# Message steps woven into the last block's projections, with x2 stored by halves of its columns and engine shares set by phase

## The chip, the cores and the metric

The kernel runs on one core of one Trainium2 chip. The metric is the device time of one execution in microseconds; lower is better. A core has five engines that run in parallel, each with its own instruction queue: TensorE (PE, matmuls and transposes into PSUM), VectorE (DVE), ScalarE (ACT), GpSimd (POOL) and SyncE (SP), which here mostly issues DMAs. An instruction waits at the head of its engine's queue until what it needs is there, and everything behind it on that engine waits with it.

## The reference

Four images of 128x128 pixels with 128 channels, in fp32, go through four residual layers, each on a group-normalised input (32 groups of 4 channels):

```python
x = x + relu(deform_conv(gn(x), offset(gn(x)), w_def))          # layer 0
x = x + scan_layer(gn(x), W)                                    # layer 1
x = x + messages(gn(x), Wself, Wm, Wk)                          # layer 2
x = x + triangle(gn(x), ...)                                    # layer 3

# layer 1: over image rows, new = row + relu(conv1d(previous new, W of 9 taps))
# layer 2
z_self = einsum('bmkd,hd->bmkh', x, Wself)
z_m = einsum('bmd,hd->bmh', sum(x, axis=2), Wm)[:, :, None, :]
z_k = einsum('bkd,hd->bkh', sum(x, axis=1), Wk)[:, None, :, :]
out = z_self + z_m + z_k
# layer 3
xn = layer_norm(x)
left = (xn @ left_w + left_b) * sigmoid(xn @ lgate_w + lgate_b)
right = (xn @ right_w + right_b) * sigmoid(xn @ rgate_w + rgate_b)
out_gate = sigmoid(xn @ ogate_w + ogate_b)
out = einsum('bkjd,bkid->bijd', left, right)
out = (layer_norm(out, onorm_g, onorm_b) * out_gate) @ to_out_w + to_out_b
```

## The kernel before

Channels lie on the 128 partitions. The kernel is a sequence of stages. `deform_layer` does layer 0 and `scan_layer` does layer 1 for all four images (batches) together; in both, a scheduler decides the order of the instructions on each engine. `message_terms` then makes the small operands of layer 2. `last_layers` does layer 2's messages and layer 3 batch by batch; there the order is written out by hand: each engine runs its instructions in the order in which the Python code emits them.

**`scan_layer`** steps through the 128 rows of the images. For a row, PE transposes four 128x128 blocks of x1 (`x1T_ps`, L1064), ACT applies the norm (`rowT`, L1068), PE convolves the carried row in two halves of two batches each (`both_ps` L1099, `own_ps` L1104 and L1110), ACT copies `both_ps` to `shared` (L1124), and DVE forms `total` (L1126), the new carry (L1129), differences for the next row (L1078) and the layer's result `x2c` (L1136). After every fourth row, a boundary of which there are 32, DVE takes `bn_stats` (L1144) and row sums (L1148, `sum_w`), POOL adds column sums (L1150, `sum_h`), and ACT's queue issues one store per batch to the HBM tensor `x2T` (L1147), four rows of 128 columns for each partition.

**`message_terms`** folds layer 2's group norm, a scale s and a shift t for each channel and batch, into its operands: `ws` (Wself scaled, plus the identity for the residual) and `z`, the row and column terms of the messages.

**`last_layers`** keeps one batch in SBUF as `X` (128x128x128 fp32) and its projections in `T`. It is written as Python generators; each `yield` ends a step, and the main loop at its end calls them in turns:

- `messages(b)`: 16 steps of 8 rows. A step loads `x2c` from x2T (SP), has POOL add the row and column terms (`zc`, L1332), does two matmuls (L1345), and DVE adds them into X (L1349) and takes two `bn_stats` (L1354). Loads and zc are fetched two steps ahead; x2c and zc share four buffers.
- `scaled(b)`: statistics of X to the operands of the next norm; eight 1-MB stores of X to `x3T` (the residual for the end).
- `normed(b)`: 16 blocks of 8 rows, `centred` by two matmuls (L1435), with two ACT passes per block, the squares (L1441) and the centred X (L1444). For every 16 rows a generator `divided` turns the mean of squares into a standard deviation (L1401), sends it through HBM (`stdT`) to spread it over partitions, takes the reciprocal (L1409), stores it (L1411) and loads it again, broadcast to all partitions (`rwide`, L1417), in two halves; each half is multiplied into X by two DVE instructions of 128x512 (L1424). Each step of `normed` advances every open `divided` by one step.
- `multiplied(b, q)`, for the four quarters q of the channels (called q0 to q3): 16 projection steps (8 matmuls and every second time one for the gate; a sigmoid on ACT L1497; two multiplies on DVE L1500), then eight product steps (four matmuls L1519 and a copy by ACT L1523). A projection step reads eight of X's first-axis slices, in order; the gates go to HBM (`gateT`).
- `given_out(b)`: layer 3's output norm, gate and projection for the 32 groups of four columns, k from -6 to 32. It works two batches' stages at once: it belongs to batch b but runs between the steps of batch b+1. A full step has DVE statistics (L1546), now and then a group of `scales` (L1562 to L1570, with a square root on ACT L1568), four normalisations `u` (ACT L1615 or POOL L1613), four transposes (L1585), y on ACT (L1587), the gate multiply (L1588, on POOL, and on DVE for the last batch), eight matmuls (L1596, L1600), and a copy of the result by ACT (L1617). x3 and the gate come in and the result goes out by DMAs on SP's queue.

The main loop before: while messages(b) has steps, given_out takes eight; three in scaled; two in normed, whose last steps run into the first projections; 24 in the projections of q0 to q2; three in q3. Messages of batch b+1 begin at n = 15 in q3, where n counts the steps of `multiplied`:

```python
if q + 1 == NQ:
    if n < 6 and n % 2:
        step(out_of)
    if n == 15:
        if b + 1 < B:
            msgs = messages(b + 1)
            step(msgs)
    elif n > 16 and n % 2:
        step(msgs)
```

So four of 16 message steps lie beside q3's products, and 12 follow them. After the last batch's q3, given_out(3) runs alone.

Of the kernel before, what the change touches and what calls it, by code (L numbers as in the profile page):

```python
# [19 lines left out]
P = 128  # L20
B = 4
# [989 lines left out]
def scan_layer(tc, c, small, x1, w, norms, x2T):  # L1011
# [18 lines left out]
    with ExitStack() as ctx:  # L1030
# [55 lines left out]
        for y in range(S):  # L1086
# [54 lines left out]
            if i == RB - 1:  # L1141
                y0 = y + 1 - RB
                for b in range(B):
                    nc.vector.bn_stats(  # L1144
                        stats[:, b, y // RB, :], x2c[:, b].rearrange("p h w -> p (h w)")
                    )
                    nc.scalar.dma_start(x2T[b, :, y0 : y + 1, :], x2c[:, b])  # L1147
# [74 lines left out]
def message_terms(tc, c, keep, work, counted, w2, outb):  # L1222
# [4 lines left out]
    wself, wm, wk = w2  # L1227
    ws = keep.tile([P, B, P], F32, name="ws")
    z = keep.tile([P, 2, B, S], F32, name="z")
    with tc.tile_pool(name="l2ps", bufs=1, space=PSUM) as psum:  # L1230
# [17 lines left out]
        nc.vector.scalar_tensor_tensor(t, mean, -1.0, s, ALU.mult, ALU.mult)  # L1248
        for b in range(B):
            nc.vector.scalar_tensor_tensor(  # L1250
                ws[:, b], wself, s[:, b : b + 1], c.ident, ALU.mult, ALU.add
            )
        tsum = work.tile([P, B], F32, name="tsum")
        nc.vector.tensor_scalar(tsum, t, float(S), None, ALU.mult)
        msg = work.tile([P, 2, B, S], F32, name="msg")
        for n, sums in enumerate((sum_w, sum_h)):
            for by, op in ((s, ALU.mult), (tsum, ALU.add)):
                nc.vector.tensor_tensor(
                    msg[:, n], sums if op is ALU.mult else msg[:, n],
                    by.unsqueeze(2).to_broadcast([P, B, S]), op,  # L1260
                )
        twide = work.tile([P, B, S], F32, name="twide")
        nc.vector.tensor_copy(twide, t.unsqueeze(2).to_broadcast([P, B, S]))
        pm = psum.tile([P, B, S], F32, name="row_ps")
        nc.tensor.matmul(pm, lhsT=wm, rhs=msg[:, 0], start=True, stop=False)
        nc.tensor.matmul(pm, lhsT=wself, rhs=twide, start=False, stop=True)
        pk = psum.tile([P, B, S], F32, name="column_ps")
        nc.tensor.matmul(pk, lhsT=wk, rhs=msg[:, 1], start=True, stop=True)

        nc.vector.tensor_scalar(z[:, 0], pm, outb, None, ALU.add)  # L1270
        nc.scalar.copy(z[:, 1], pk)
# [3 lines left out]
def last_layers(tc, c, terms, w, x2T, out, x3T, gateT, stdT):  # L1275
# [9 lines left out]
    with ExitStack() as ctx:  # L1285
# [36 lines left out]
        def messages(b):  # L1322

            stats = xs[b] = one.tile([P, S // 4, 6], F32, name="stats3")
            got = []

            def fetch(y0):
                if y0 < S:
# [428 lines left out]
```

## Time and profile before

| | |
|---|---|
| median of 3 runs | 5456.43 us (5450.79 to 5477.0) |
| the profiled execution's own time | 5459.8 us |
| its span | 5458.1 us |
| layer 0 | 0 to 3120 us |
| scan layer | 3120 to 3952 us |
| message terms | 3952 to 3973 us |
| last layers | 3973 to 5458 us |
| in these, from the first messages of one batch to those of the next | 358 us (batches 1 to 2 and 2 to 3) |
| last batch's given_out alone | 5335 to 5458 us |

The profile is one execution; the span is what lies between its first and last instruction, and the remaining 1.7 us lie around it. Within one batch's period of 358 us (batch 1's q0 to batch 2's), the phases take 53 (q0), 57 (q1), 57 (q2), 47 (q3's projections), 63 (its products and the next messages), 30 (scaled) and 51 us (normed up to the first projection). A group of the profile gives a line, an engine and an operation, its operands and shape, how often it ran, its busy time and the mean ns of one, and after the second bar how long the engine stood idle just before it and for what. A line of the waits view gives the engine and line that waited, what it waited for, total us, times and the longest.

### The profile page before, as it was taken

The page shows a single profiled execution, that of the slowest core. Times are in us where ns is not written, and L with a number is a line of the kernel's source. Part 1 is how long each engine was busy: PE and PEld are TensorE (multiplying, and loading weights), DVE is VectorE, ACT ScalarE, POOL GpSimd, SP SyncE. Part 2 cuts the span into 40 slices and gives each one's busy share as a digit, 9 for nine tenths or more (in the row PEclk, how much of TensorE's full clock was granted, in tenths as well). Part 3 has the DMA queues.
Part 4 walks back from the last instruction along what each step waited for, and adds up shares of the span by engine and source line. Part 5 has one row for each costly group of instructions (what it writes and reads, how often), then busy time and mean ns, then how long its engine had stood idle before and what let it go on. Part 6 is the DMA issues. An engine that isn't in the chain of part 4 may idle for free. (4 is left out here: it accounts for less than half of the span.)

```text
span 5458.1 us, 162832 instructions
## 1 busy us (share of the span) xinstructions
PE 4887.5 (90%) x68890; PEld 4229.0 (77%) x68890; DVE 3237.4 (59%) x8389; ACT 2536.8 (46%) x5206; POOL 1137.0 (21%) x1013
## 2 busy tenths in 40 slices
PE   1898999999999998989999799999969699798897
PEld 1787788788888787877899699999928478396596
DVE  4676666666666655665545466666654654546445
ACT  1554454544554444545544233333234375573666
POOL 4222121210221201212100011111120232323222
PEclk9999998999999999999999899999989899899998
DMA  5776666665666665665644322222141553554535
GB/s 151 162 161 145 138 139 140 142 150 103 142 138 130 157 120 107 150 130 126 129 85 90 73 82 78 78 84 83 61 166 64 174 179 122 195 172 145 191 132 193
DMA packets 1273817, 710.67 MB, mean 130 GB/s; under 512 B 845645, under 2 KB 1112174, under 8 KB 1263862
## 3 DMA queue, kind: packets, MB, share of 16 engines
q1 hardware_dynamic: 1243538, 658.56, 47.8%
q10 hardware_dynamic: 29540, 41.60, 2.2%
q8 instruction: 545, 8.93, 0.7%
q14 instruction: 194, 1.59, 0.1%
HBM read 417.28 MB, written 282.55 MB: 128 GB/s over the span
## 5 line engine op out<-in xcount | busy, mean ns | idle before, releaser
L606 PE MATMUL conv_ps<-ring,wdef 128*128 128x192 f32 (+2 forms) x7632 | 1301.2, 320 | 8.7 <-DVE x1c L576 6.6
L514 DVE TENSOR_TENSOR m<-t_ps,tent 128x390 f32<-128x390 f32 x1548 | 806.7, 557 | 783.2 <-ACT tent L512 767.5
L606 PEld LDWEIGHTS conv_ps<-ring,wdef 128*128 128x128 f32 x7632 | 1146.9, 195 | 127.1 <-issue 64.6
L512 ACT COPY tent<-t_ps 128x390 f32<-128x390 f32 x1560 | 690.5, 487 | 654.7 <-PE t_ps L498 642.2
L498 PE MATMUL t_ps<-parts_of,spread 57*64 57x99 bf16 (+1 forms) x12384 | 742.5, 275 | 169.0 <-DVE m L514 149.3
L523 PE MATMUL v_ps<-m,pixels 60*64 60x108 f32 (+1 forms) x22704 | 812.5, 264 | 19.0 <-DVE m L514 11.1
L498 PEld LDWEIGHTS <-spread 57*64 57x64 bf16 x12480 | 578.7, 125 | 313.0 <-issue 265.7
L523 PEld LDWEIGHTS v_ps<-m,pixels 60*64 60x64 f32 x22704 | 673.0, 137 | 69.8 <-DVE m L514 24.7
L549 ACT COPY ring<-v_ps 128x432 f32<-128x432 f32 x1032 | 505.1, 525 | 445.7 <-PE v_ps L523 444.8
L420 POOL TENSOR_TENSOR off<-off,koff 72x512 f32<-72x512 f32 x128 | 162.7, 1271 | 1768.2 <-DVE off L417 1768.2
L1500 DVE TENSOR_TENSOR T<-pair_ps,sig 128x256 f32<-128x256 f32 x512 | 282.6, 594 | 390.8 <-ACT sig L1497 390.7
L1110 PEld LDWEIGHTS own_ps<-diff,wconv 128*128 128x128 f32 x4064 | 493.6, 191 | 13.1
L1492 PEld LDWEIGHTS pair_ps<-wcat,X 128*128 128x128 f32 x4096 | 472.7, 192 | 38.1 <-issue 29.1
L1110 PE MATMUL own_ps<-diff,wconv 128*128 128x128 f32 x4064 | 494.6, 273 | 0.0
L1492 PE MATMUL pair_ps<-wcat,X 128*128 128x128 f32 x4096 | 481.5, 276 | 5.2 <-DVE T L1500 3.1
L506 PE MATMUL t_ps<-parts_of,spread 57*64 57x130 bf16 x9288 | 454.5, 225 | 0.0
L1150 POOL TENSOR_TENSOR sum_h<-sum_h,x2c 128x512 f32<-128x512 f32 x128 | 162.4, 1268 | 1150.5 <-DVE x2c L1136 684.8
L438 DVE SCALAR_TENSOR_TENSOR parts<-off,parts 72x512 bf16<-72x512 f32 x384 | 296.1, 771 | 153.5 <-ACT parts L430 147.7
L1068 ACT ACTIVATE rowT<-x1T_ps,t_x,s_x 128x128 f32<-128x128 f32 x512 | 208.2, 571 | 323.2 <-PE x1T_ps L1064 320.8
L506 PEld LDWEIGHTS <-spread 57*64 57x64 bf16 x9312 | 318.9, 108 | 0.1
L1497 ACT ACTIVATE sig<-pair_ps 128x512 f32<-128x512 f32 x256 | 152.1, 598 | 253.5 <-DVE T L1500 104.6
L1099 PE MATMUL both_ps<-carry,wsum 128*128 128x128 f32 x2032 | 268.3, 273 | 1.1 <-DVE carry L1133 1.1
(195 smaller groups left out, 6609.8 us busy)
## 6 DMA issues: line engine op xcount, KB each, us to landing
pixels<-tab SPq DMA_DIRECT2D x688, 123.8 KB
parts_of<-off SPq DMA_DIRECT2D x1032, 55.7 KB
off<-parts SPq DMA_DIRECT2D x64, 891.0 KB
tab<-rows SPq DMA_DIRECT2D x384, 128.0 KB
xin<-in_x_dram SPq DMA_DIRECT2D x128, 256.0 KB
x<-x1c SPq DMA_DIRECT2D x32, 1024.0 KB
x1rows<-x SPq DMA_DIRECT2D x128, 256.0 KB
x2T<-x2c ACTq DMA_DIRECT2D x128, 256.0 KB
```

The source lines that it names most:

```text
L438: nc.vector.scalar_tensor_tensor(parts[:, NSPLIT + i, h : h + RO, 2 : S + 2], off, 0.0, part, ALU.is_gt, ALU.mult,)
L498: nc.tensor.matmul(tp[h : h + HALF, 0, 0:n].rearrange("p (r c) -> p r c", c=PADW)[:, :, i:PADW:RX], lhsT=spread[0:k, kx // 2, i, h : h + H ...
L506: nc.tensor.matmul(tp[h : h + HALF, 1, i * PADW : (i + 1) * PADW], lhsT=spread[HALF : HALF + k, kx // 2, first + i, h : h + HALF], rhs=src ...
L512: nc.scalar.copy(tent[:, 0:n], tp[:, 0, 0:n])
L514: nc.vector.tensor_tensor(m, *pair, ALU.mult)
L523: nc.tensor.matmul(to[p1 : p1 + HALF], lhsT=pix[p0 : p0 + LANES, xb, :], rhs=m[p0 : p0 + LANES, :, RX * xb : RX * xb + w], start=True, sto ...
L549: nc.scalar.copy(to, bodies[side])
L606: nc.tensor.matmul(pc[:, at : at + rows, x0:x1], lhsT=wdef[:, side, k, :], rhs=v[:, :, k if v.shape[2] == NK else kx, x0 + kx : x1 + kx], ...
L1099: nc.tensor.matmul(both, lhsT=wsum[:, j, :], rhs=old[h][:, 1, :, j : j + V], start=(j == 0), stop=(j == NJ - 1),)
L1110: nc.tensor.matmul(own[:, n], lhsT=wt[:, 2 * j + n, :], rhs=diffs[h][:, n, :, j : j + V], start=False, stop=(n == 1 and j == NJ - 1),)
L1492: nc.tensor.matmul(pj[:, j], lhsT=X[:, j0 + j, :], rhs=w.wcat[:, q * 4 * DQ : (q + 1) * 4 * DQ], start=True, stop=True,)
L1500: nc.vector.tensor_tensor(to, pj[:, :, e].rearrange("p j d -> p d j"), sig[:, :, e].rearrange("p j d -> p d j"), ALU.mult,)
```

## The change

`x2T` gets a further axis: [B, P, 2, S, S/2], so that each half of the columns lies together. Each store of `scan_layer` is split into two.

`message_terms` no longer scales the row and column sums. The scale goes into copies of the weights (per batch, Wm on POOL and Wk on ACT), the shift into one small matmul with `wshift` = S (Wm + Wk) + Wself, made at the start by `message_weights`. Results come per batch from one PSUM tile.

`messages(b)` steps over 16 rows x 64 columns, first half of X's first axis and then the second. Because q3's projections have passed the first half by then, messages of b+1 can start inside them: they are fetched at n = 7, eight steps run with n = 8 to 15 and three with n = 17, 20 and 23; five are left after q3.

`divided` waits one step more between the rwide loads and the multiplies, and the second multiply of each half goes to POOL. `centred` puts every second block's centred X on DVE. The loop of normed makes 25 steps before the projections, with given_out at 7, 15 and 23; given_out takes seven steps beside the messages, three in scaled and three in normed.

`given_out` always takes scales in groups of four columns' groups, a step before they are used, with statistics six steps ahead. The four `u` of a step are shared by phase: all on ACT up to k = 5 and two each on ACT and POOL later (before three and one); for the last batch one on ACT and three on POOL (before two and two).

```diff
-                    nc.scalar.dma_start(x2T[b, :, y0 : y + 1, :], x2c[:, b])
+                    for n in range(2):
+                        nc.scalar.dma_start(
+                            x2T[b, :, n, y0 : y + 1, :], x2c[:, b, :, n * V : (n + 1) * V]
+                        )
...
+def message_weights(tc, work, w2):
+
+    nc = tc.nc
+    wt = []
+    for v, name in zip(w2, ("wself", "wm", "wk")):
+        t = work.tile([P, P], F32, name=name)
+        nc.scalar.dma_start(t, v)
+        wt.append(t)
+    wself, wm, wk = wt
+    shifted = work.tile([P, P], F32, name="wshift")
+    nc.vector.tensor_tensor(shifted, wm, wk, ALU.add)
+    nc.vector.scalar_tensor_tensor(shifted, shifted, float(S), wself, ALU.mult, ALU.add)
+    return wself, wm, wk, shifted
...
+        same_ps = psum.tile([P, B], F32, name="same_ps")
+        nc.tensor.matmul(same_ps, lhsT=shifted, rhs=t, start=True, stop=True)
+        same = work.tile([P, B], F32, name="same")
+        nc.vector.tensor_scalar(same, same_ps, outb, None, ALU.add)
+        scaled = work.tile([P, B, 2, P], F32, name="wscaled")
         for b in range(B):
-            nc.vector.scalar_tensor_tensor(
-                ws[:, b], wself, s[:, b : b + 1], c.ident, ALU.mult, ALU.add
-            )
-        tsum = work.tile([P, B], F32, name="tsum")
-        nc.vector.tensor_scalar(tsum, t, float(S), None, ALU.mult)
-        msg = work.tile([P, 2, B, S], F32, name="msg")
-        for n, sums in enumerate((sum_w, sum_h)):
-            for by, op in ((s, ALU.mult), (tsum, ALU.add)):
-                nc.vector.tensor_tensor(
-                    msg[:, n], sums if op is ALU.mult else msg[:, n],
-                    by.unsqueeze(2).to_broadcast([P, B, S]), op,
-                )
-        twide = work.tile([P, B, S], F32, name="twide")
-        nc.vector.tensor_copy(twide, t.unsqueeze(2).to_broadcast([P, B, S]))
-        pm = psum.tile([P, B, S], F32, name="row_ps")
-        nc.tensor.matmul(pm, lhsT=wm, rhs=msg[:, 0], start=True, stop=False)
-        nc.tensor.matmul(pm, lhsT=wself, rhs=twide, start=False, stop=True)
-        pk = psum.tile([P, B, S], F32, name="column_ps")
-        nc.tensor.matmul(pk, lhsT=wk, rhs=msg[:, 1], start=True, stop=True)
-
-        nc.vector.tensor_scalar(z[:, 0], pm, outb, None, ALU.add)
-        nc.scalar.copy(z[:, 1], pk)
+            sb = s[:, b : b + 1]
+            nc.vector.scalar_tensor_tensor(ws[:, b], wself, sb, c.ident, ALU.mult, ALU.add)
+            nc.gpsimd.tensor_scalar(scaled[:, b, 0], wm, sb, None, ALU.mult)
+            nc.scalar.activation(scaled[:, b, 1], wk, AF.Copy, scale=sb)
+            pm = psum.tile([P, 2, S], F32, name="added_ps")
+            for n, sums in enumerate((sum_w, sum_h)):
+                nc.tensor.matmul(
+                    pm[:, n], lhsT=scaled[:, b, n], rhs=sums[:, b], start=True, stop=True
+                )
+            nc.vector.tensor_scalar(z[:, 0, b], pm[:, 0], same[:, b : b + 1], None, ALU.add)
+            nc.scalar.copy(z[:, 1, b], pm[:, 1])
     return ws, z
...
+            RB, V = 2 * JB, S // 2
...
+            todo = [(n, y0) for n in range(2) for y0 in range(0, S, RB)]
             got = []
 
-            def fetch(y0):
-                if y0 < S:
-                    x2c = four.tile([P, JB, S], F32, name="x2c", tag="wide")
-                    nc.sync.dma_start(x2c, x2T[b, :, y0 : y0 + JB, :])
-                    zc = four.tile([P, JB, S], F32, name="zc", tag="wide")
+            def fetch(i):
+                if i < len(todo):
+                    n, y0 = todo[i]
+                    x2c = four.tile([P, RB, V], F32, name="x2c", tag="wide")
+                    nc.sync.dma_start(x2c, x2T[b, :, n, y0 : y0 + RB, :])
+                    zc = four.tile([P, RB, V], F32, name="zc", tag="wide")
                     nc.gpsimd.tensor_tensor(
-                        zc, z[:, 0, b, y0 : y0 + JB].unsqueeze(2).to_broadcast([P, JB, S]),
-                        z[:, 1, b].unsqueeze(1).to_broadcast([P, JB, S]), ALU.add,
+                        zc, z[:, 0, b, y0 : y0 + RB].unsqueeze(2).to_broadcast([P, RB, V]),
+                        z[:, 1, b, n * V : (n + 1) * V].unsqueeze(1).to_broadcast([P, RB, V]),
+                        ALU.add,
                     )
                     got.append((x2c, zc))
 
             fetch(0)
-            fetch(JB)
+            fetch(1)
             yield
-            for y0 in range(0, S, JB):
+            for i, (n, y0) in enumerate(todo):
                 x2c, zc = got.pop(0)
                 pz = pair()
                 for h in range(2):
                     nc.tensor.matmul(
-                        pz[:, h], lhsT=ws[:, b], rhs=x2c[:, 4 * h : 4 * h + 4],
+                        pz[:, h], lhsT=ws[:, b], rhs=x2c[:, JB * h : JB * (h + 1)],
                         start=True, stop=True,
                     )
+                x = X[:, n * V : (n + 1) * V]
                 nc.vector.tensor_tensor(
-                    X[:, :, y0 : y0 + JB].rearrange("p w h -> p h w"),
-                    pz.rearrange("p n (h w) -> p (n h) w", w=S), zc, ALU.add,
-                )
-                for h in range(0, JB, 4):
+                    x[:, :, y0 : y0 + RB].rearrange("p w h -> p h w"),
+                    pz.rearrange("p n (h w) -> p (n h) w", w=V), zc, ALU.add,
+                )
+                for h in range(2):
                     nc.vector.bn_stats(
-                        stats[:, (y0 + h) // 4, :], X[:, :, y0 + h : y0 + h + 4]
-                    )
-                fetch(y0 + 2 * JB)
+                        stats[:, 2 * i + h, :], x[:, :, y0 + JB * h : y0 + JB * (h + 1)]
+                    )
+                fetch(i + 2)
                 yield
...
                     rws.append((j1, rw))
                 yield
-                for j1, rw in rws:
+                yield
+                for (j1, rw), engine in zip(rws, (nc.vector, nc.gpsimd)):
                     flat = X[:, j1 : j1 + 4, :].rearrange("p j i -> p (j i)")
-                    nc.vector.tensor_tensor(flat, flat, rw, ALU.mult)
+                    engine.tensor_tensor(flat, flat, rw, ALU.mult)
...
-                nc.scalar.activation(
-                    X[:, j1 : j1 + JB, :].rearrange("p j i -> p (j i)"), flat, AF.Identity, bias=ct
-                )
+                to = X[:, j1 : j1 + JB, :].rearrange("p j i -> p (j i)")
+                if engine is nc.scalar:
+                    nc.scalar.activation(to, flat, AF.Identity, bias=ct)
+                else:
+                    nc.vector.tensor_scalar(to, flat, ct, None, ALU.add)
                 return sq
...
-            sqs = [centred(0)]
+            sqs = [centred(0, nc.scalar)]
             yield
             for j0 in range(0, S, 2 * JB):
-                sqs.append(centred(j0 + JB))
+                sqs.append(centred(j0 + JB, nc.vector))
                 advance()
                 yield
                 if j0 + 2 * JB < S:
-                    sqs.append(centred(j0 + 2 * JB))
-                    advance()
-                    yield
+                    sqs.append(centred(j0 + 2 * JB, nc.scalar))
+                advance()
+                yield
                 pv = single()
...
-            groups = {1: 0, 4: 1, 8: 4} if alone else {4: 0, 8: 4}
-            groups.update({16: 8, 24: 16, 32: 24})
-            counts = {-6: (0,), -5: (1,), -4: (2,), -3: (3,), -2: (4,), -1: (5,), 0: (6,), 1: (7,),
-                      2: (8,), 3: (9,), 4: (10, 11), 5: (12, 13), 6: (14, 15)}
-            counts.update({k: (k + 9,) for k in range(7, 23)})
+            groups = {k + 4: k for k in range(0, NS_, 4)}
+            if alone:
+                groups.update({1: 0, 4: 1})
             st, factors, us, ys, gates, x3s, outs = {}, {}, {}, {}, {}, {}, {}
...
-                for i in counts.get(k, ()):
-                    statistics(i)
-                    if i + 1 in groups:
-                        scales(groups[i + 1], i + 1)
+                if k + 6 < NS_:
+                    statistics(k + 6)
+                    if k + 7 in groups:
+                        scales(groups[k + 7], k + 7)
...
-                        if j >= (2 if alone else 3):
+                        if j >= (1 if alone else 4 if k < 6 else 2):
...
             n = 0
             while step(msgs):
-                if n < 4 or n % 2:
-                    step(out_of)
+                step(out_of, 2 if n < 2 else 1)
                 n += 1
             for _ in scaled(b):
                 step(out_of)
-            for n, _ in enumerate(normed_start := normed(b)):
-                if n in (6, 14):
+            norm = normed(b)
+            for n in range(25):
+                step(norm)
+                if n in (7, 15, 23):
                     step(out_of)
-                if n == 23:
-                    break
-
-            msgs = iter(())
+
+            msgs = messages(b + 1) if b + 1 < B else iter(())
             for q in range(NQ):
                 for n, _ in enumerate(multiplied(b, q)):
-                    step(normed_start)
-                    if q + 1 == NQ:
-                        if n < 6 and n % 2:
+                    step(norm)
+                    if q + 1 < NQ:
+                        if n in (1, 3, 5, 7, 9, 11, 15, 20):
                             step(out_of)
-                        if n == 15:
-                            if b + 1 < B:
-                                msgs = messages(b + 1)
-                                step(msgs)
-                        elif n > 16 and n % 2:
-                            step(msgs)
-                    elif n in (1, 3, 5, 7, 9, 11, 15, 20):
+                        continue
+                    if n in (1, 3, 5):
                         step(out_of)
+                    if 7 <= n < 16 or n in (17, 20, 23):
+                        step(msgs)
             out_of = given_out(b)
...
-    x2T = dram.tile([B, P, S, S], F32, name="x2T")
+    x2T = dram.tile([B, P, 2, S, S // 2], F32, name="x2T")
```

## The prediction

> **What bounds the kernel now.** I read the page from the top: busy time, slices, then stretches.
>
> ```profile
> PE 4887.5 (90%) x68890; PEld 4229.0 (77%) x68890; DVE 3237.4 (59%) x8389; ACT 2536.8 (46%) x5206; POOL 1137.0 (21%) x1013
> PE   1898999999999998989999799999969699798897
> DMA  5776666665666665665644322222141553554535
> ```
>
> TensorE (PE) is busy 90% of the span. The lower digits from the 30th slice on lie in the last layers, the stage the change mostly edits. The windows view gives that stage's third batch by phase (engines as PE, PEld, DVE, ACT, POOL; then clock, DMA share, GB/s):
>
> ```profile
> 4763.00:4816.00 53.00, 48.56 (x385) 43.75 (x386) 32.95 (x73) 32.85 (x58) 18.15 (x20) 1.00 0.61 201
> 4816.00:4873.00 57.00, 57.00 (x468) 52.81 (x467) 28.45 (x74) 42.52 (x77) 14.83 (x17) 1.00 0.44 150
> ...
> 4930.00:4976.00 46.00, 45.52 (x363) 41.29 (x361) 17.24 (x32) 21.88 (x38) 6.33 (x5) 1.00 0.22 79
> 4976.00:5040.00 64.00, 45.79 (x164) 23.58 (x164) 58.31 (x82) 13.91 (x24) 32.36 (x21) 0.92 0.50 159
> 5040.00:5070.00 30.00, 10.46 (x55) 9.93 (x56) 10.35 (x39) 10.28 (x20) 5.10 (x6) 0.61 0.94 359
> 5070.00:5121.00 51.00, 45.49 (x162) 16.96 (x161) 21.27 (x50) 43.28 (x51) 13.21 (x15) 0.96 0.43 137
> ```
>
> In order: q0, q1, q3 of the projections (PE full, DVE idle for most of q3); products and next batch's messages (DVE 58 of 64 us); scaled (DMA 0.94, 359 GB/s); normed (no engine full by count of work: few instructions, long waits). The groups of messages, scaled and normed (4620 to 4763) give prices, and the waits there name the chains:
>
> ```profile
> L1349 DVE TENSOR_TENSOR X<-pair_ps,zc 128x1024 f32<-128x1024 f32 x16 | 30.6, 1911 | 4.7 <-PE pair_ps L1345 4.7
> L1354 DVE BATCH_NORM_STATS2 stats<-X 128x6 f32<-128x512 f32 x32 | 20.6, 686 | 0.5
> L1424 DVE TENSOR_TENSOR X<-X,rwide 128x512 f32<-128x512 f32 x20 | 13.5, 691 | 17.2 <-DMA rwide<-stdT 12.5 <-ACT X L1444 3.9 <-PE pair_ps L1435 0.6
> L1588 POOL TENSOR_TENSOR y<-y,gate 128x512 f32<-128x512 f32 x8 | 10.4, 1298 | 42.2 <-ACT y L1587 27.2 <-DMA gate<-gateT 15.0
> ```
> ```profile
> DVE rstd L1409 <- DMA rstd<-stdT: 27.7, 1, 27.7
> ...
> POOL y L1588 <- DMA gate<-gateT: 15.0, 1, 15.0
> ...
> DVE X L1424 <- DMA rwide<-stdT: 12.5, 8, 3.4
> ```
>
> The first is one long wait: DVE has nothing from scaled (4696) until normed's first standard deviations are back from HBM. The second is a gate load queued behind scaled's eight x3T stores (8 MB). The third is normed's loop: a broadcast load of what has just been stored. The scan layer is PE alone:
>
> ```profile
> 3120.00:3952.00 832.00, 832.00 (x6998) 819.08 (x6998) 565.93 (x1404) 255.13 (x750) 158.56 (x125) 1.00 0.25 78
> ```
>
> **What the Trainium skill says.** "VectorE: DVE Perf Modes", section on the TRN2 errata, gives an fp32 tensor_tensor as (N+151)/0.96 ns: 691 ns at N=512; L1424 measures 691. "GPSIMD Engine Reference", §3.1, has GpSimd 1.96 times slower at N=2048, and §8 says it shares its SBUF interfaces with DVE instructions of two SBUF inputs; here a 128x512 multiply takes 1298 ns on POOL (1.9 times), and the last batch's DVE y multiply beside POOL 879 against 691. "DMA: Bandwidth & Descriptors", "Why small descriptors are slow", has a 256-byte descriptor lose 27%: bounded below by the trace. "Perfetto Trace Analysis", "Optimization Strategy", says that regimes with different bounds can gain by interleaving; q3 and messages are such a pair.
>
> **The change part by part**, against the profiled execution's 5459.8 us (3.4 over the median 5456.4, or 0.06%; so the sum is taken off either).
>
> *Scan.* 128 stores of 128 runs of 2048 B become 256 of 512 runs (256 B). On ACT's queue two stores took 0.81; eight a group then cost 3.3, or 4.1 at the 0.51 that x1rows' loads of 512 runs take, against 1.6. ACT works 255 of 832 us. DMA: x2T packets took 10.5% of 16 x 832 us over 17,856 packets, 78 ns; x1rows' 512-B packets 29. 131,072 packets of 256 B at 15 to 29 ns take 2.0 to 3.8 ms of engine time for 1.4: share 0.25 becomes 0.29 to 0.43, hidden under PE. But the scheduler reorders: on the built order, at each of 31 four-row boundaries DVE does both totals (L1126) before both carries (L1129), PE two rows of transposes at once, and five stores instead of two precede the first shared copy (L1124). Before, DVE's reduce (L1148, 2.27 us from 3503.28) ends at 3505.46, the copy at 3503.26: 2.2 us of slack for three more issues (1.2 to 1.5). The first carry now waits for the second own_ps, about 3506.9, plus total 0.42 and carry 0.43: 3507.8, where PE is ready at 3506.66 + 0.88 = 3507.5. 0.3 x 31 = **+9**; bounds +3 and +20.
>
> *Message terms* (3952 to 3972). Out: four 128x512 passes (0.69 each) and a copy. In: per batch ws, two scalings (POOL, ACT), two matmuls and two z writes, on one psum buffer. Four serial rounds of about 1.8 us against some 8: **-1** (-3 to +1).
>
> *Weaving*, three transitions. A message step costs DVE 1.91 + 2 x 0.69, 3.15 apart in the timeline; a projection step two T multiplies, 1.19. Woven: 4.34, taken as 4.45, since PE needs 2.23 + 1.72 = 3.95 and POOL's zc (1.9), loads and stores have room (q3: POOL 6 of 46, DMA 0.22; zc precedes no y multiply in q3, the loads stand on SP behind gate stores of the same step). Eight steps: 8 x (4.45 - 2.23) = +17.8. Products start 0.7 later and carry three messages instead of four: -0.7. Afterwards 12 messages and 8 given_out steps (12 x 3.15 + 8 x 1.2 = 47.4, measured 49) become 5 and 7: 24; -25. Together **-8 each, -24**. Bounds: at 3.95 per step -12; at 5.5 (zc, TT and the T multiplies in series, 1.9 + 1.9 + 1.2, and 0.5 of handing over) 0.
>
> *Scaled.* The stall is kept: the gate still stands behind the same stores. POOL gives its u to ACT (10 of 30 busy): **-3** in three batches (-9 to +6).
>
> *Normed.* ACT gives eight X centrings (1.13 each) to DVE, 21 busy of 51, and POOL takes every second 128x512 multiply. The loop per 16 rows (multiply, reciprocal, store, load) is about 7.0 us in the timeline (std at 4058.8, 4066.4, 4072.9, 4079.1). The next reciprocal's store now waits on SP behind a load whose buffer POOL's multiply must free; the extra yield leaves the load a step more to land. I take the loop as unchanged; what shrinks is the rest left for q0, one multiply chain less: -2 for the first batch, -3 for the others: **-11**. Bounds: -30 if the yield breaks the loop, +15 if POOL's 1.3 (0.6 over DVE's) enters it in half the cases.
>
> *q0 to q2 and products:* nothing. PE is 57.00 of 57.00 in q1. The three more scale groups per batch bring ACT table loads (1.28 each) and waits into ACT's 14 idle us; one such group lies in that window, where DVE waits 5 us for ACT's root, without a PE gap. u moves to POOL there, 15 of 57 busy. Were the cover gone: 3 x 2.6 x 3 = +23.
>
> *Last batch alone.* From the waits (5350 to 5445):
>
> ```profile
> POOL u L1613 <- DVE nm L1570: 38.8, 5, 10.4
> PEld one_ps L1585 <- ACT u L1615: 38.0, 42, 8.3
> ```
>
> A step takes 2.41 us: ACT y 0.78, two u of 0.60, x 0.57. With three u on POOL (3 x 0.56 = 1.7) ACT falls to 1.95, and memory becomes next: 768 KB at 359 GB/s is 2.19. Some 24 free steps x 0.2 = -5; scales a step ahead but seven groups instead of four: 7 x 2.75 = 19.3 for the 19.5 of before. **-5** (-14 to +3).
>
> Sum: 9 - 1 - 24 - 3 - 11 - 5 = **-35**, or 5424.8 profiled, **5421** at the median.
>
> **Rivals.** *Normed's loop breaks* (the load lands before its turn, one round trip less in most chunks: some 1.3 us of 7 over 32 chunks, -40, in place of -11, and the tail at its better bound): -35 - 29 - 9 = -73, 5383. For it: the 12.5 us of rwide waits; against: the chain store, load, multiply stays serial. *The weave gives nothing* (woven steps at 5.5): -35 + 24, and scan at +15 instead of +9: -5, 5451. For it: zc waited 56 us for X; against: two pairs of buffers and DVE's slack. *POOL in normed's loop* (slower): both halves' multiplies enter the chain at 1.3 x 1.3 contention (879/691), 1.7 us for 0.69: +2 us per 16 rows x 32 = +64 in place of -11: +40, 5496. It decides from 1.6 us per 16 rows on ((27 + 24)/32). For it: memset and both halves queue on POOL; against: DVE's half runs at the same time. *The stores don't do what they say*: at 1.1 us an issue scan alone would lose 2.5 a boundary, +77; x1rows' 0.51 speaks against it, and I count it with the slower case.
>
> **How the numbers follow.** A measurement can tell about 0.5%, 27 us. Likeliest case 0.45, mostly under 5429; loop broken 0.14; weave lost 0.23; slower 0.18. Faster = 0.8 x 0.45 + 0.14 = 0.50; same = 0.2 x 0.45 + 0.23 = 0.32; slower 0.18. The likeliest case alone spans 5400 to 5440; the range, 5378 to 5484, adds the other cases down to half of the slower one.
>
> **What would show it.** Right: q3 longer by some 18 us, the stretch from products to scaled shorter by some 26; PE still 1.00 in the scan with its length within +3 to +20; normed's std interval near 7; tail steps near 2.2. Wrong: woven steps over 5.2, std intervals over 8.5 with POOL's X multiply as releaser, or a shared copy in the scan waiting for stores.

## The result, and the profile after

The change made the kernel slower: 5498.22 us median of 7 runs (5472.29 to 5501.18) against 5456.43 (5450.79 to 5477.0); the ratio is 1.0063, interval 1.0043 to 1.0084. The forecast was 5421. The span of the profiled execution grew from 5458.1 to 5499.1. The stages below are cut on PE, at the first and last transpose of the scan, the first matmul of the messages and of normed, and the first product of a quarter. A quarter's products therefore count with the row that follows: "normed and q0" ends at q0's first product, "q1 and q2" runs from there to q2's first product.

| us | before | after | change | forecast |
|---|---|---|---|---|
| layer 0 | 3105.2 | 3106.6 | +1.4 | 0 |
| scan, first to last transpose | 841.4 | 853.6 | +12.2 | +9 |
| message terms | 26.2 | 26.1 | -0.1 | -1 |
| first batch's messages and scaled | 57.0 | 58.7 | +1.7 | 0 |
| normed and q0, four batches | 410.6 | 483.8 | **+73.2** | **-11** |
| q1 and q2, four batches | 428.9 | 443.0 | **+14.1** | **0** |
| q3, and from its products to the next normed | 465.4 | 409.8 | **-55.6** | **-27** |
| last batch from its last products | 123.3 | 117.6 | -5.7 | -5 |

Layer 0 is the same in all kernels here, and its length in their single profiled executions lay between 3086.9 and 3109.1 us. Totals of single runs therefore carry some 20 us that are not the edit's; I compare stages. Where two kernels below have the same code in a stage, its length differs by up to 0.2 us in q1 and q2, and by 1.5 to 3.0 us in normed and q0 (changed and e6, e4 and e16, e11 and e13).

The windows view of the third batch after, with cuts at q0, q1, q3's projections and the stretches after them (the columns are PE, PEld, DVE, ACT, POOL, then clock, DMA share and GB/s):

```profile
4725.00:4785.00 60.00, 48.79 (x180) 19.24 (x180) 18.16 (x34) 38.00 (x48) 20.41 (x19) 0.90 0.38 116
4785.00:4851.00 66.00, 54.85 (x384) 48.30 (x383) 40.91 (x81) 33.20 (x57) 33.97 (x38) 0.90 0.55 177
4851.00:4910.00 59.00, 57.05 (x464) 52.52 (x464) 30.36 (x76) 40.89 (x70) 18.90 (x24) 1.00 0.44 144
4969.00:5033.00 64.00, 61.59 (x402) 48.21 (x401) 39.24 (x53) 22.44 (x39) 20.67 (x13) 1.00 0.39 120
5033.00:5070.00 37.00, 27.47 (x117) 16.15 (x115) 33.43 (x55) 12.83 (x23) 15.43 (x9) 0.91 0.66 217
5070.00:5091.00 21.00, 11.91 (x53) 10.57 (x54) 12.16 (x36) 11.21 (x23) 4.07 (x4) 0.70 0.97 379
```

The first two rows are normed (60 us, before 51 to 52) and q0 (66, before 53): PE is now busy for 55 of q0's 66 us, at a clock of 0.90. The third is q1: PE no longer fills it (57.05 of 59). The fourth is the woven q3, where DVE and PE are busy together, 39 and 62 of 64 us, and the last two are what is left between q3 and normed: 58 us in place of 93.

What holds normed and q0 up, from the groups and the waits between 4725 and 4851:

```profile
L1445 POOL TENSOR_TENSOR X<-X,rwide 128x512 f32<-128x512 f32 x16 | 20.3, 1270 | 16.9 <-DMA rwide<-stdT 14.0 <-PE one_ps L1490 1.9 <-PE one_ps L1601 1.0
L1445 DVE TENSOR_TENSOR X<-X,rwide 128x512 f32<-128x512 f32 x16 | 14.7, 940 | 0.0
L1469 DVE TENSOR_SCALAR X<-pair_ps,ct 128x1024 f32<-128x1024 f32 x8 | 10.1, 1264 | 21.3 <-ACT sq L1462 21.3
L1421 ACT ACTIVATE std<-one_ps,eps 128x512 f32<-128x512 f32 x8 | 5.5, 689 | 14.7 <-POOL X L1445 10.3 <-DMA stdT<-std 3.7 <-ACT X L1467 0.7
```

The same `std` before (4711 to 4816):

```profile
L1401 ACT ACTIVATE std<-one_ps,eps 128x512 f32<-128x512 f32 x8 | 5.6, 697 | 3.7 <-DVE X L1424 2.8 <-DMA rstd<-stdT 0.8 <-PE one_ps L1467 0.2
```

POOL's multiply takes 1270 ns for DVE's 691. The 940 ns of the DVE multiply are a mean of two kinds: over the whole execution 49 of the 64 ran clear of POOL's multiply and took 684 ns on average, the other 15 took 1567. The two halves of a pair seldom ran side by side; in 44 of 64 pairs POOL's started first. From the first start to the last end a pair took 2.41 us in the median, before 1.36. DVE's centring waits 21.3 us for ACT's squares. The last row is a wait that has grown: ACT's `std` shares four buffers with `rwide` and waits for a multiply to free one, before 2.8 us for DVE's, now 10.3 for POOL's. Behind it on ACT stand the next squares.

### The profile page after: what moved, and what is told of

Read it like the earlier page. It is cut to its first block, busy times and chain, and to the rows that moved or that the text cites. A ratio compares the mean times of both kernels' runs of the same rounds, so it can differ in the third digit from the quotient of the medians.

```text
span 5499.1 us, 163068 instructions
## 1 busy us (share of the span) xinstructions
PE 4923.4 (90%) x68902; PEld 4257.7 (77%) x68902; DVE 3263.9 (59%) x8405; ACT 2492.0 (45%) x5131; POOL 1269.4 (23%) x1161
## 5 line engine op out<-in xcount | busy, mean ns | idle before, releaser
L523 PEld LDWEIGHTS v_ps<-m,pixels 60*64 60x64 f32 x22704 | 672.0, 137 | 71.4 <-DVE m L514 21.3
L1515 PEld LDWEIGHTS pair_ps<-wcat,X 128*128 128x128 f32 x4096 | 486.7, 196 | 79.5 <-issue 65.5
L1515 PE MATMUL pair_ps<-wcat,X 128*128 128x128 f32 x4096 | 498.0, 280 | 34.7 <-DVE T L1523 28.9
```

What stands on the lines that cost most here:

```text
L523: nc.tensor.matmul(to[p1 : p1 + HALF], lhsT=pix[p0 : p0 + LANES, xb, :], rhs=m[p0 : p0 + LANES, :, RX * xb : RX * xb + w], start=True, sto ...
L1515: nc.tensor.matmul(pj[:, j], lhsT=X[:, j0 + j, :], rhs=w.wcat[:, q * 4 * DQ : (q + 1) * 4 * DQ], start=True, stop=True,)
```

## The experiments

All kernels start from the changed one unless stated. Of the three edits in normed, the POOL multiply alone, with the extra yield kept, was not tried; the two were separated in the other order.

**e2, one yield in `divided`.**

```diff
                 yield
-                yield
                 for (j1, rw), engine in zip(rws, (nc.vector, nc.gpsimd)):
```

> The changed kernel without the second yield in divided; POOL still takes the second multiply, DVE still every second centring. In the changed kernel normed and q0 together take 105.8, 127.2, 126.1, 124.9 us in the four batches (before: 96.8, 104.6, 105.2, 104.1; 73 us more in all). Theory A (POOL's multiply, 1.27 for 0.69, sits in the round-trip chain): most of the 73 us stays, standard deviations 8.5 us apart, profiled time 5480 to 5505. Theory B (the extra yield: rwide buffers are held a step longer, so SP's loads and ACT's std wait for them): most of it goes, std 6.5 to 7 apart, 5425 to 5450. Theory C (DVE's centring behind ACT's squares): little changes here, as A.

Measured: 5462.05 us. normed and q0 take 457.3 us, 26.5 less than with the yield. In the first batch the last five standard deviations come 6.7 to 7.6 us apart, with the yield 8.6 to 8.9; in later batches there remain gaps of 12. Neither theory takes all: undoing the yield alone gives back 26.5 us, and 46.7 of the 73.2 stay. The waits of SP's own queue show why a further step of waiting costs time. In the changed kernel (4725 to 4785):

```profile
SPq L1437 <- DMA rwide<-stdT: 9.1, 5, 3.3
SPq L1437 <- POOL X L1445: 7.0, 5, 1.5
...
SPq L1431 <- DVE rstd L1429: 1.5, 1, 1.5
```

and without the yield (4699 to 4758):

```profile
SPq L1431 <- DVE rstd L1429: 10.5, 6, 4.2
SPq L1437 <- DMA stdT<-rstd: 8.2, 5, 3.6
SPq L1437 <- DVE X L1444: 4.6, 2, 4.2
SPq L1437 <- POOL X L1444: 3.0, 3, 1.3
```

L1437 is the issue of an rwide load, L1431 the store of a reciprocal. With the yield the head of SP's queue is a rwide load that waits for a buffer, whose last user waits for its own load or for POOL (9.1 + 7.0 us); the next chunk's reciprocal, 8 KB on which the next round trip hangs, is done and its store stands behind that load. Without the yield SP stands waiting for that reciprocal instead (10.5 us), so it goes out as soon as it exists. The delay can be read directly: from the end of a reciprocal to the issue of its store pass 1.0 to 1.8 us in seven of the eight rounds of every batch with the yield, 9.4 to 10.0 us a batch, and without it 0.0 us in all rounds but the last (0.0 to 1.4). Within a round the order of SP's queue is the same in both kernels, so what differs is how long these loads wait for their buffers. More buffers were not tried.

**e9, one yield and both multiplies on DVE.**

```diff
-                for (j1, rw), engine in zip(rws, (nc.vector, nc.gpsimd)):
+                for (j1, rw), engine in zip(rws, (nc.vector, nc.vector)):
```

> The changed kernel without the extra yield and with both multiplies on DVE; DVE keeps every second centring. normed and q0 over four batches so far: before 410.7, changed 484.0, without the yield 457.3, all three edits undone 426.0 us. Theory (the POOL multiply costs by itself, 1.27 for 0.69 twice a chunk in the round trip): 457.3 falls to between 425 and 440; total 5430 to 5447. Rival (only the yield and the centring cost; POOL's multiply runs beside DVE's): it stays at 450 or more; total 5455 to 5465.

Measured: 5447.28 us, normed and q0 437.4. Against e2 that is 19.9 us for POOL's multiply, within the theory's bounds. DVE's multiplies are back at 692 ns, and a pair takes 1.33 us in the median where e2's takes 2.32.

**e3, all centring on ACT.**

```diff
-                sqs.append(centred(j0 + JB, nc.vector))
+                sqs.append(centred(j0 + JB, nc.scalar))
```

> The changed kernel with all sixteen centrings on ACT, as before; extra yield and POOL multiply kept. Theory C (DVE's centring waits for ACT's squares, and the chain's multiplies and reciprocals queue behind it): most of the 73 us in normed and q0 goes, 5430 to 5450. Theories A and B: at most 15 of the 73 us go, 5483 to 5505; normed itself longer or equal, since ACT gets eight passes of 1.11 us back.

Measured: 5496.18 us, normed and q0 476.4: 7.4 us less. Theory C fails as the main cause, but handing ACT's work to the idler DVE cost time and saved none.

**e4, all three undone.**

> The changed kernel with all three edits in normed undone (one yield, both multiplies on DVE, centring on ACT); weaving, groups, shares and the 25 steps kept. All theories: normed near 52, q0 near 53 us, 65 to 73 us less than the changed kernel: 5425 to 5435. If normed and q0 stay above 115 us a batch, the cause is none of the three (the 25 steps and the places of given_out, or POOL's u).

Measured: 5438.3 us, normed and q0 426.0, that is 57.8 of the 73.2 us back, where 65 to 73 were expected, and 11.4 less than e9, which has only DVE's centring on top. Stepwise: yield 26.5, POOL multiply 19.9, centring 11.4, and 15.4 remaining. The shares depend on the order of undoing: the centring gives 7.4 undone first (e3) and 11.4 undone last. SP's waits in this kernel (4690 to 4744) have the healthy form: first of all for the reciprocal, and no rwide behind a buffer for more than half a microsecond.

```profile
SPq L1431 <- DVE rstd L1429: 15.5, 6, 3.5
...
SPq L1437 <- DVE X L1444: 0.5, 2, 0.3
```

**e10, given_out's steps beside the messages and normed placed as before, on e4.**

```diff
-                step(out_of, 2 if n < 2 else 1)
+                step(out_of, 2 if n < 3 else 1)
...
-            for n in range(25):
+            for n in range(24):
                 step(norm)
-                if n in (7, 15, 23):
+                if n in (6, 14):
```

> The kernel with all three edits of normed undone (5438.3), and its given_out steps placed as before: eight beside the messages, two in normed (n = 6 and 14), 24 steps of normed. Theory P (the third given_out step in normed, queued on ACT, DVE, PE and SP between the round trips, is what keeps normed and q0 of the later batches at 110 to 113 us for 104 to 105 before): 5 to 7 us less in each of three batches, of which 2 to 3 us come back beside the messages: total 5425 to 5432. Theory U (u all on ACT, the busiest engine of normed): no change, 5435 to 5441.

Measured: 5468.4 us, slower. normed and q0 fall by 7.4 us (418.6; 48 us of normed with 60 of q0), half or less of what theory P expected, but the stretches between q3 and normed rise from 58.5 to 69.5 us, where it expected 2 to 3. The timeline of SP's queue shows what one more given_out step does there. e10:

```profile
5041.61 0.34 SPq L1592 DMA_DIRECT2D out_dram<-x  x1
...
5042.96 8.66 SPq L1395 DMA_DIRECT2D x3T<-X  x8
```

The changed kernel:

```profile
5058.76 0.43 SPq L1638 DMA_DIRECT2D gate<-gateT  x1
5059.23 15.47 SPq L1395 DMA_DIRECT2D x3T<-X  x8
5074.80 1.17 SPq L1593 DMA_DIRECT2D out_dram<-x  x1
```

With eight steps the first result's store (`out_dram`) stands ahead of the eight x3T stores, and it waits for given_out's own chain: the first x3T store goes out at 5043.0, when the last message addition has begun (5041.9). With seven the first four go out from 5059.2 on, 10.6 us ahead of the last addition (5069.8), since the first half of X, which they read, is complete by then. So the halves let half of the 8 MB pass under the last messages, but only where nothing slow is ahead of the stores on SP.

**e15 and e16, not woven, on e4.** Messages of the next batch are fetched at n = 15 and stepped four times beside the products, as before:

```diff
-                    if 7 <= n < 16 or n in (17, 20, 23):
+                    if n == 15 or n in (17, 19, 21, 23):
```

> The kernel with normed's edits undone (span 5436.1), but messages of the next batch fetched at n = 15 and stepped at 17, 19, 21, 23 as before: four steps beside the products, twelve after q3. q3 plus the stretch up to the next normed took 410.1 us over the batches there (before 465.4). Theory (weaving itself is worth 8 us a transition; the rest of the gain is the overlap of the x3T stores with messages, and one given_out step moved into normed): q3 back at 46.9 a batch, 24 to 30 us more in all than with weaving, about 435; total 5460 to 5468. Rival (the whole gain of 18 us a transition is the weave): 465, total 5488 or more.

Measured: 5486.46 us, but given_out now took a step beside each of the twelve messages, and q1 and q2 fell to 106.5 us from 118.4 a batch. The run mixes the two moves and says nothing of the weave's own worth. e16 takes a step at seven of the twelve:

```diff
-                step(out_of, 2 if n < 2 else 1)
+                if b == 0 or n in (0, 1, 2, 3, 5, 7, 9):
+                    step(out_of)
```

> As the unwoven kernel, but with seven given_out steps beside the twelve messages that follow q3, so that nothing else moves (the unwoven run took a step per message, 14, and its q1 and q2 lost six). The kernel with normed's edits undone has 410.1 us in q3 and the stretches up to the next normed, over the batches, before 465.4. Halves and one step fewer are kept, so the x3T stores can still start early. Theory (weaving itself 8 us a transition): 434, span near 5460. Rival (all of the 18 us a transition is the weave): 465, span near 5490. A value in between gives the weave's own share.

Measured: 5466.25 us; q3 and the stretches take 442.7 us, woven (e4) 410.1, before 465.4. So weaving itself is worth 32.6 us or 10.9 a transition, between theory and rival, and what else changed there (halves with earlier stores, one given_out step less, the u shares) another 22.7, 7.6 a transition. Here too the stores go out before the last addition, at 4675.5 against 4682.7.

**e11, before's scale groups, on e4.** The scale groups of `given_out` and the times of its statistics as in the kernel before.

```diff
-            groups = {k + 4: k for k in range(0, NS_, 4)}
-            if alone:
-                groups.update({1: 0, 4: 1})
+            groups = {1: 0, 4: 1, 8: 4} if alone else {4: 0, 8: 4}
+            groups.update({16: 8, 24: 16, 32: 24})
...
-                if k + 6 < NS_:
-                    statistics(k + 6)
-                    if k + 7 in groups:
-                        scales(groups[k + 7], k + 7)
+                for i in counts.get(k, ()):
+                    statistics(i)
+                    if i + 1 in groups:
+                        scales(groups[i + 1], i + 1)
```

> The kernel with all three edits of normed undone, and the scale groups, their timing and the statistics of before (groups of up to 32 columns, roots a step or more earlier in the count). In the changed kernel q1 and q2 take 59.2 us with two groups each, before 56.9 with one. Theory G (each group's two table loads and its root hold ACT's sigmoid, 2.3 us per extra group): q1 and q2 back at 56.9, 14 us in six blocks, and about 2 each in three q0: total 5418 to 5425; the tail, 116.6 in that kernel, gives back up to 6. Rival (the u on POOL, two for one): q1 and q2 stay at 59.2.

Measured: 5430.07 us; q1 and q2 take 428.2 us over the four batches for 442.8, so the 14 us belong to the groups and their times. The last batch's tail is 125.2 us for 116.6: there the small groups pay. The timelines show the difference of the two cases. Before, the one root of a quarter falls late among the products, 10 us after the last projection:

```profile
4821.92 1.28 ACT L1568 ACT_TABLE_LOAD   x1
4823.22 0.32 ACT L1568 ACTIVATE rs<-rs,eps 128x32 f32<-128x32 f32 x1
...
4826.28 1.54 ACT L1523 COPY T<-one_ps 128x512 f32<-128x512 f32 x3
4827.84 1.28 ACT L1497 ACT_TABLE_LOAD   x1
```

No sigmoid is due there, and PE does not stop. After, a quarter has two roots. One falls among the projections:

```profile
4879.90 1.28 ACT L1584 ACT_TABLE_LOAD   x1
4882.18 0.31 ACT L1584 ACTIVATE rs<-rs,eps 128x16 f32<-128x16 f32 x1 [1.00 <-DVE rs L1581]
...
4883.97 1.28 ACT L1520 ACT_TABLE_LOAD   x1
4885.26 1.09 ACT L1520 ACTIVATE sig<-pair_ps 128x512 f32<-128x512 f32 x2
```

From the first load to the next sigmoid pass 5.4 us, more than the 4.5 or so that two projection steps last, and the two `pair_ps` buffers hold no more. The other root falls where the projections end and the products begin; PE needs a `one_ps` buffer there that ACT's copy `x` frees, and the copy stands behind the root. PE's stops at the two, from the timelines of ACT and PE:

```profile
4853.38 0.31 ACT L1584 ACTIVATE rs<-rs,eps 128x16 f32<-128x16 f32 x1 [1.29 <-DVE rs L1581]
4855.19 2.05 PE L1542 MATMUL one_ps<-T 128*128 128x128 f32 x16 [1.31 <-ACT x L1633]
...
4887.13 1.13 PE L1515 MATMUL pair_ps<-wcat,X 128*128 128x128 f32 x8 [0.64 <-DVE T L1523]
```

These 1.31 and 0.64 us are PE's only stops in the stretch, and most of the 2.35 by which it grew; the larger is not at the sigmoids.

**e12, u three to ACT and one to POOL, on e4.**

```diff
-                        if j >= (1 if alone else 4 if k < 6 else 2):
+                        if j >= (1 if alone else 3):
```

> The kernel with all three edits of normed undone, and u shared three to ACT and one to POOL in every phase before the last batch's tail, as before. Rival to theory G (u's share costs the 2.3 us in q1 and q2): back at 56.9, total 5420 to 5426. Theory G: 59.2 stays or grows. Theory U (u all on ACT lengthens normed): normed and q0 of the later batches 4 to 6 us shorter each, total 5422 to 5428 with q1 at 59.2. Theory P: no change, 5435 to 5441.

Measured: 5449.28 us; q1 and q2 447.1 (442.8), normed and q0 428.3 (426.0). In q1 and q2 the changed shares are better; the 2.3 us of normed and q0 lie within what equal code differs by. Theory U and the rival to G fail.

**e6, whole x2T stores.** The old layout and one store per batch, the messages reading columns out of it:

```diff
-                    nc.sync.dma_start(x2c, x2T[b, :, n, y0 : y0 + RB, :])
+                    nc.sync.dma_start(x2c, x2T[b, :, y0 : y0 + RB, n * V : (n + 1) * V])
```

> The changed kernel with x2T in its old layout and one store per batch in the scan; the messages load their 16 rows x 64 columns from it, in runs of 256 bytes instead of 4 KB. The scan, first transpose to last, takes 853.6 us in the changed kernel and 841.3 before. Theory (the second store moves the scheduler's order at the boundaries): the scan is back at 841 to 842, 12 us gained; and the messages' loads, 2048 descriptors each, cost something: woven part unchanged if they land within two steps (8.9 us), total 5485 to 5490. Rival (small packets, not the order): the scan gains the same 12, since they go too; the built order tells these apart, and if the scan stays at 853 both are wrong.

Measured: 5488.71 us; the scan is back at 841.9. The first batch's messages and scaled, which run bare, take 66.0 us instead of 58.7 with loads in runs of 256 bytes; the woven ones hide them (q3 and the stretches 409.9 against 409.8). The run takes order and packets away together, so it does not part them by itself.

**e13, the combination.** e4 with e6's layout and, in the first three batches, e11's groups.

> The changed kernel with what the runs charged taken back: normed's three edits undone, whole x2T stores, and before's scale groups in the first three batches (the last batch keeps the changed ones, since its tail took 125.2 us with before's and 116.6 with these). Kept: weaving by halves, u shares, placing. If the parts add up: 5436.1 (span) - 11.7 (scan) - 14.6 (q1, q2) = 5410, plus 0 to 7 for messages(0), whose loads in 256-byte runs took msg0 from 58.7 to 66.0: time 5408 to 5420, some 0.8% under before. If a part only moved (ACT or the queues meet the next limit), above 5425.

Measured in 5 rounds: 5397.85 us (5395.69 to 5415.46), ratio to the kernel before 0.9888, interval 0.9869 to 0.9907. It is 1.1% faster than the kernel before. Its total lies below the 5408 to 5420 expected because layer 0 took 3086.9 us in it and 3102.1 in e4. Without layer 0 its span is 83 us under the changed kernel's, 44 under that of before, and 24.8 under e4's, for 26.3 less 0 to 7 expected: the parts add up.

**e14, the first four x3T stores between the message steps, on e13.**

```diff
+                    if 8 <= i < 12:
+                        rows_ = slice((i - 8) * 16, (i - 7) * 16)
+                        nc.sync.dma_start(x3T[b, :, rows_, :], X[:, rows_, :])
...
-            for j0 in range(0, S, 16):
+            for j0 in range(S // 2, S, 16):
```

> The combined kernel, with the first four of the eight x3T stores of scaled issued between message steps 9 to 12, when the first half of X is complete. In the changed kernel the stores were issued at 5059.2 with the last message addition at 5069.8: eleven us of their traffic lay beside messages, which the halves make possible, and the stretch from q3's products to the next normed fell by 34 us a batch where 25 was reckoned. Theory (scaled is bound by those 8 MB, 22 us at 359 GB/s, and what they delay): another 6 to 11 us less in each of three transitions and in messages(0): 5370 to 5395. Rival (after the overlap scaled is bound by its serial chain of small operations, or the early stores hold up message loads on SP): within 8 us of the combined kernel.

Measured in four executions: 5405.39 us (5403.22 to 5413.31), ratio 0.9894 (0.9877 to 0.9912), not told apart from e13. The stretches are 6.1 us shorter in all (170.6 for 176.7), but the first batch's messages and scaled 6.4 longer (68.8 for 62.4). There three of the four early stores held SP for 4.1 to 4.4 us each, with the next message's load behind them, and the message steps after them took 4.5 to 6.2 us instead of 3.2 or so. Whether the queue or the shared DMA is to blame, no run parts. The total agrees with the rival; without layer 0 the span is 5.2 us under e13's.

## Why the prediction was wrong

**Scan and message terms: right.** +12.2 for +9, -0.1 for -1. In the scan's window PE is 827.32 of 832 us busy after, DMA 0.32 for 0.25. The packets came to 18.3% of 16 engines x 832 us over 130,944 packets, 18.6 ns each, within the bounds of 15 and 29. The loss lies at the boundaries, as the forecast had it: four rows take 27.0 us for 26.6, and at each boundary PE now stops, mostly 0.14 us, for DVE's carry, where it did not stop before. Between 3125 and 3945 PE stops for nothing else, and for no DMA. That the two extra issues on ACT, and not the smaller packets, moved the order is the forecast's reading; e6 takes both away.

**Last batch: the number right, its split not.** -5.7 for -5. The forecast gave all of it to the u shares and nothing to the groups (19.3 us for 19.5). With the new shares and before's groups (e11) the tail took 125.2 us, not less than the 123.3 of before; the small groups brought 8.6. The other runs with the changed tail lie between 115.4 and 120.2. That the total fits is in part luck.

**Weaving: right in kind, a little under-sized.** The woven step takes 4.15 and 4.9 us in turn (4.5 on average, 4.45 forecast) and q3 grew by 16.7 (17.8 forecast). e16 gives 10.9 us a transition for 8.

**Scaled: the step failed.** The forecast wrote "The stall is kept" and gave -3. What it missed is that halves complete X early, so half of scaled's stores overlap with messages, if SP lets them: 22.7 us together with the step moved away and the u shares (e16 against before).

**Normed: the step that sank the forecast.** The step is "I take the loop as unchanged", with -11; measured +73.2. The forecast had named the very wait, "The next reciprocal's store now waits on SP behind a load whose buffer POOL's multiply must free", and put it at nothing, set off by the yield that "leaves the load a step more to land". In the runs the yield makes this wait: the store goes out 1.0 to 1.8 us late in seven of eight rounds with it, and not late without it but for a last round here and there (e2). The three edits were judged a relief or free, and each cost: the yield 26.5; the POOL multiply, in the chain only in a bound of +15 and in the slower rival, 19.9; the DVE centring, booked as relief for ACT, 11.4. Of the forecast's signs of being wrong this one came: in the first batch standard deviations 8.6 to 8.9 us apart, with waits of `std` for POOL's multiply.

The slower rival named the place, and its +2 us per 16 rows is what the pairs grew by (2.41 for 1.36, two pairs). But only 19.9 us of its 64 reached the stage's length, and the larger part was the yield, which it did not count; that its total of 5496 comes within 3 us is luck. Of the remaining 15.4 us, the third given_out step and 25th normed step account for 7.4 (e10), before's groups for 3.2, which is hardly told from nothing (e11); the rest stays open.

**q1 and q2: the step failed** on "one such group lies in that window [...] without a PE gap". That group's root came late in the products; the changed kernel's roots fall at the start of the products and among the projections, where PE stops 1.31 and 0.64 us. "Were the cover gone" had +23; it was +14.1.

In all, what gained brought 61 us (55.6 + 5.7 + 0.1), where the forecast had 44 ahead of the scan's +9; but two parts that were to gain 11 or cost nothing took 87 (73.2 + 14.1).

## What to carry to other kernels

A loop that hangs on a round trip can pay for an instruction in it and for a buffer held longer while the engines are idle: here spare busy time was not spare time, and a load that waited for a buffer at the head of an in-order queue delayed the short store behind it on which the next round hung. When a forecast names such a wait, it should price it. Before calling an added instruction covered, look at the same phase and not at the same window: a root late in the products cost PE nothing, one among the projections 0.64 us and one between the two 1.31. And a layout that completes a buffer in halves can pay beyond the interleaving it was made for, through stores that start early, if the queue that issues them has nothing slow in front.

## What was not expected of the hardware

A DVE multiply of 128x512 fp32 and one on POOL hardly ran at the same time. Where they met, DVE's was lengthened by nearly as much as the two overlapped: by 0.49 us for 0.64, by 0.98 for 1.12, and in this pair of e2, begun within 0.03 us, by 1.15 for 1.26:

```profile
4063.47 1.84 DVE L1444 TENSOR_TENSOR X<-X,rwide 128x512 f32<-128x512 f32 x1
4063.50 1.26 POOL L1444 TENSOR_TENSOR X<-X,rwide 128x512 f32<-128x512 f32 x1
```

Two such multiplies in a row on DVE take 1.38 us. Three DVE multiplies of the changed kernel took 4.08 to 4.09 us, while four POOL instructions ran one after the other (a multiply by the gate, two u, a multiply by rwide). POOL's memset did not do this: with 0.48 us shared, DVE's multiply took 684 to 686 ns. A centring of 128x1024 out of PSUM took DVE 1264 ns and ACT 1110.
